# A graph layer's front on one core: the node table split into bf16 parts through TensorE, in spans of three nodes, under one written order

## The chip, the core and the metric

The kernel runs on one core of a Trainium2 chip. The core has TensorE (PE, matrix products, with its weight loads shown as PEld), VectorE (DVE), ScalarE (ACT), GpSimd (POOL) and SyncE (SP), which here only issues DMAs. The metric is the device time of one execution in microseconds (us); lower is better.

## The reference

One layer of a graph network over 12 500 nodes with 128 features and 200 000 edges of 4 types. The edges come sorted by destination, and low node numbers have far more of them (the destinations are drawn as the square of a uniform number).

```python
def reference(x, src, dst, edge_type_4, L0_gnn_W, L0_gnn_b):
    h = jnp.maximum(_layernorm(x, axis=-1), 0.0)      # per node, no learned scale
    xs = h[src]
    msgs = 0
    for i in range(4):
        mask = (edge_type_4 == i)[:, None]
        msgs = msgs + jnp.where(mask, xs @ W[i] + b[i], 0.0)
    return x + jax.ops.segment_sum(msgs, dst, num_segments=12500)
```

## The kernel before

**Data.** Edges are taken in chunks of 128, 1 563 in all. The normalised rows h are written once to a table in DRAM, `htab`. A row there is 768 bytes: the float32 value split into three bf16 parts, since TensorE's bf16 products of the three parts add up to nearly the float32 one. Node p·98 + j lies on partition p at place j (`NW` = 98 places; the last partition is short, so nodes from place `NL` = 54 on are loaded in three pieces, L186 to L188, and those before in one, L183).

**The dense part.** The first 512 chunks belong to the few nodes with many edges. For them the kernel counts, per destination, how often each source and type occurs (`count`: two one-hot tiles L924/L925 on VectorE, a product L936 on TensorE, the counts out through ScalarE L939), and multiplies the counts with the whole table (`multiply`, L976, with the table read back as `hs`). It needs *slots*: each destination's edges, one to a row. `prep_dense` prepares the edges' sources, types and destinations (L343 on), `make_slots` finds the slots: `first_chunk` (one-hots of L787, products of L796), then `pick_out` (L787, products L825 and L828, masks L837 to L842 on VectorE), then `unpack` (L851 on), then sums of the bias by L895 and L897.

**The other chunks.** The first 48 of them, three *raw groups* of `G` = 16 (`RAW` = 3), do not wait for the table: GpSimd gathers rows of x itself (`gather_raw`, L509, tile `hx`), VectorE takes their statistics (L431), ScalarE normalises them (L451), and TensorE sums them by destination and type in float32 (`add_up_raw`, L609 to L620). All later chunks take rows of the table by GpSimd gathers (`gather`, L525, tile `hm`, two chunks in each of 20 buffers), which need the whole table written. A group is summed by one-hots of its destinations (L542), products L559, a copy L562, the weights L586, and added into a ring (L637).

**Order.** In the loop (from L1182) the three engines PE, DVE and ACT run in the order in which the program writes their instructions (`tc.manual_schedule`), and the dense work is dealt out between the groups' parts by a pace. In front of the loop a scheduler orders the instructions; SP and POOL are always ordered by it. The first gathers of `hm` are spread by gates: the k-th buffer's first gather also waits for the k-th of a list of marked instructions (`marks`, in `make_slots` and `add_up_raw`).

**The table.** It is made in 13 blocks of up to `XG` = 8 nodes per partition. `look` loads a block (three ahead) and takes statistics: L431 for each node, then L434 to L439 on VectorE, a square root L440 on ScalarE, L441 and L442. `table` normalises each node with ScalarE (L451) and splits the block:

```python
nc.scalar.copy(h3[:r, :n, 0, :], h[:r, :n, :])                              # L471
nc.vector.tensor_sub(h[:r, :n, :], h[:r, :n, :], h3[:r, :n, 0, :])          # L473
nc.scalar.copy(h3[:r, :n, 1, :], h[:r, :n, :])                              # L474
nc.vector.tensor_sub(h3[:r, :n, 2, :], h[:r, :n, :], h3[:r, :n, 1, :])      # L476
nc.sync.dma_start(htab[...][:, j0:j1, :], h3[...])                          # L477
```

Beside it stand the loads and small preparations: `heads` and `brow` (where a chunk's sums go in the ring, L1105 and L1106), and the bias, split into bf16 parts and laid out row by row by twelve DMAs of 256 bytes (L1140).

Of the kernel before, what the change touches and what calls it, by code (L numbers as in the profile page):

```python
# [35 lines left out]
F32 = mybir.dt.float32  # L36
# [12 lines left out]
P = 128  # L49
EPS = 1e-5  # L50
XG = 8
# [21 lines left out]
def kernel(  # L73
# [269 lines left out]
    def prep_dense():  # L343
# [6 lines left out]
        n = slice(0, DENSE)  # L350
        nc.vector.tensor_single_scalar(first1, di[:, n, 0], 1.0, op=ALU.add)
# [5 lines left out]

        lo = prep.tile([P, QB, P], I32, name="sf")
        nc.vector.tensor_single_scalar(lo[:, n], si[:, n], float(-(-(1 << 16) // NW)), op=ALU.mult)
        nc.vector.tensor_single_scalar(lo[:, n], lo[:, n], 16, op=ALU.arith_shift_right)  # L360
        bk = prep.tile([P, QB, P], F32, name="rel")
        nc.vector.scalar_tensor_tensor(bk[:, n], lo[:, n], float(-NW), si[:, n], op0=ALU.mult, op1=ALU.add)
        over = prep.tile([P, QB, P], F32, name="key")
        nc.vector.tensor_single_scalar(over[:, n], bk[:, n], -0.5, op=ALU.is_lt)
        nc.vector.tensor_sub(what[:, 1], lo[:, n], over[:, n])
        nc.vector.scalar_tensor_tensor(bk[:, n], over[:, n], float(NW), bk[:, n], op0=ALU.mult, op1=ALU.add)
        nc.vector.tensor_scalar(over[:, n], ty[:, n], 1.0, float(P), ALU.add, ALU.mult)
# [20 lines left out]
    nc.vector.tensor_copy(iota_n, iota_d)  # L388
    ones_h = prep.tile([P, P], F16, name="ones_h")
# [30 lines left out]
    looked = []  # L420

    def stats(xt, n, r, what, tag, wide=XG):

        bufs = 4 if wide == XG else 2
        sums2 = what.tile([P, wide, 2], F32, name="mv" + tag, bufs=bufs)
        var = what.tile([P, wide], F32, name="var" + tag, bufs=bufs)
        rstd = what.tile([P, wide], F32, name="rstd" + tag, bufs=bufs)
        nmr = what.tile([P, wide], F32, name="nmr" + tag, bufs=bufs)
        st = what.tile([P, wide, 2, 3], F32, name="st" + tag, bufs=3 if wide == XG else 1)
        for k in range(n):  # L430
            last = nc.vector.bn_stats(st[:r, k].rearrange("p h s -> p (h s)"), xt(k))  # L431
        looked.append(last.ins)

        nc.vector.tensor_tensor(sums2[:r, :n], st[:r, :n, 0, 1:], st[:r, :n, 1, 1:], ALU.add)  # L434
        nc.vector.tensor_tensor(var[:r, :n], st[:r, :n, 0, 1], st[:r, :n, 1, 1], ALU.subtract)
        nc.vector.scalar_tensor_tensor(
            var[:r, :n], var[:r, :n], 0.25 * D, var[:r, :n], op0=ALU.mult, op1=ALU.mult
        )
        nc.vector.tensor_tensor(var[:r, :n], var[:r, :n], sums2[:r, :n, 1], ALU.add)  # L439
        nc.scalar.activation(rstd[:r, :n], var[:r, :n], AF.Sqrt, bias=eps[:r], scale=1.0 / D)  # L440
        nc.vector.reciprocal(rstd[:r, :n], rstd[:r, :n])  # L441
        nc.vector.scalar_tensor_tensor(  # L442
            nmr[:r, :n], sums2[:r, :n, 0], -0.5, rstd[:r, :n], op0=ALU.mult, op1=ALU.mult
        )
        return rstd, nmr

    def normalize(xt, h, n, r, of):

        rstd, nmr = of
        return [  # L450
            nc.scalar.activation(h(k), xt(k), AF.Relu, bias=nmr[:r, k : k + 1], scale=rstd[:r, k : k + 1]).ins  # L451
            for k in range(n)
        ]

    seen_x = {}

    def look(j0, j1, r):
        xt = npool.tile([P, XG, D], F32, name="xt", bufs=4)
        load_nodes(xt, j0, j1)
        seen_x[j0] = xt, stats(lambda k: xt[:r, k, :], j1 - j0, r, aheads, "t")  # L460


    tabling = []

    def table(j0, j1, r):
        n = j1 - j0
        xt, of = seen_x.pop(j0)
        h = npool.tile([P, XG, D], F32, name="h")
        h3 = npool.tile([P, XG, 3, D], BF16, name="h3")
        normalize(lambda k: xt[:r, k, :], lambda k: h[:r, k, :], n, r, of)  # L470
        nc.scalar.copy(h3[:r, :n, 0, :], h[:r, :n, :])  # L471
        yield True
        nc.vector.tensor_sub(h[:r, :n, :], h[:r, :n, :], h3[:r, :n, 0, :])  # L473
        nc.scalar.copy(h3[:r, :n, 1, :], h[:r, :n, :])  # L474
        yield True
        nc.vector.tensor_sub(h3[:r, :n, 2, :], h[:r, :n, :], h3[:r, :n, 1, :])  # L476
# [4 lines left out]
    def table_steps():  # L481
        for t in list(tabling):
            if next(t, None) is None:
                tabling.remove(t)

    tables = []
    for j0, j1 in ((0, NL), (NL, NW)):
        for j in range(j0, j1, XG):
            tables.append((j, min(j + XG, j1), P))
# [60 lines left out]
    def sum_up(t0, g, rows, oh, last):  # L550
# [3 lines left out]
        for i0 in range(0, g, SG):  # L554
            i1 = min(i0 + SG, g)
            ps = s_ps.tile([P, SG, P], F32, name="ps")[:, :, :K]
# [34 lines left out]
    def add_up_raw(t0, g, rows):  # L591
        win = window_of(C0 + t0)
        K = NT * win
        oh = npool.tile([P, G, KR], F32, name="ohf", bufs=2)[:, :, :K]
# [6 lines left out]
        row = lambda k: rows(k, 0)  # L601
        done = normalize(row, row, g, P, stats(row, g, P, aheads, "r", wide=G))
        if t0:
            marks.extend(done[g // 2 - 1 :: g // 2])
        sb = spool.tile([P, G * KM], F32, name="sb")[:, : G * K].rearrange("p (g t n) -> p g t n", g=G, t=NT)
        for i0 in range(0, g, SG):
            ps = s_ps.tile([P, SG, P], F32, name="ps")[:, :, :K]
            for i in range(i0, i0 + SG):
                nc.tensor.matmul(ps[:, i - i0, :], rows(i, 0), oh[:, i, :], start=True, stop=True)  # L609
# [784 lines left out]
```

## Time and profile before

| | |
|---|---|
| time, median of 3 runs | 1667.20 us (1661.71 to 1671.48) |
| the profiled execution's own time | 1657.39 us |
| its span in the profile | 1655.6 us, mean granted clock 0.959 |
| PE / DVE / ACT / POOL busy | 81% / 62% / 36% / 63% |
| last subtraction of the table (L476) ends | 100.8 us |
| first gather from the table (L525) | 104.25 us |
| first product of the dense work (L936) | 152.3 us |

Times in a profile count from the start of the span. Lines such as L976 are lines of the kernel; a group's row names the engine, the tiles (output <- inputs), the shapes, how often it occurs, its busy time, the mean of one instruction, and the idle time of its engine just before it with what ended that. The mean of one instruction includes its latency: many in a row follow each other faster than that.

### The profile page before, as it was taken

The numbers are of one execution on the slowest core, as the hardware profiler recorded it, in microseconds if no ns is written. First come the engines' busy times: TensorE is split into PE (matmuls) and PEld (weight loads), VectorE is DVE, ScalarE is ACT, GpSimd is POOL, SyncE is SP. The second block draws the span as 40 slices with busy tenths as digits, with TensorE's granted clock in tenths as the row PEclk, the third lists the DMA queues.
The fourth block names the chain that finished last, engine by engine and source line by source line (L and its number), as shares of the span: only waits on it lengthen the run. The fifth ranks groups of instructions, "written<-read, shape, count | busy, mean of one in ns | idle before, by whom it ended". The sixth has DMA issues, their size and how long they took to land.

```text
span 1655.6 us, 30447 instructions
## 1 busy us (share of the span) xinstructions
PE 1340.6 (81%) x9644; PEld 793.0 (48%) x9644; DVE 1032.7 (62%) x5197; ACT 600.4 (36%) x1993; POOL 1035.9 (63%) x1078
## 2 busy tenths in 40 slices
PE   0275788888878888888988889888888988897985
PEld 0152455545445555454545545554544554554554
DVE  9876889776766565555656555655556554773245
ACT  7861525233242433424233342332424324224111
POOL 7737666666666666666666666666666566666660
PEclk9996699999999999999999999999999899999998
DMA  7634356655555655555555555565555555555652
GB/s 234 190 104 122 90 175 177 174 165 149 166 158 167 183 166 170 175 177 165 176 171 171 171 171 152 172 183 162 170 161 165 155 162 161 173 164 159 183 167 72
DMA packets 137188, 270.25 MB, mean 163 GB/s; under 512 B 25818, under 2 KB 73868, under 8 KB 137021
## 3 DMA queue, kind: packets, MB, share of 16 engines
q1 hardware_dynamic: 87341, 166.44, 33.7%
q0 software_dynamic: 49680, 101.81, 21.8%
q8 instruction: 76, 1.25, 0.3%
q14 instruction: 91, 0.75, 0.2%
HBM read 252.12 MB, written 16.04 MB: 162 GB/s over the span
## 4 chain that ended last, share of the span: by engine, by line
PE 75%; issue 10%; DVE 7%; POOL 3%; ACT 2%; another core or an unknown queue 1%; DMA 0%; DVEq 0%; ACTq 0%; POOLq 0%
PE pa L976 43%; PE pt L936 12%; PE py L586 7%; PE ps L559 7%; POOL hx L509 2%; DVE o L925 2%; DVE o L924 1%; ACT counts L939 1%; PE py L577 1%; PE pt L992 1%; PE pt L662 1%; DVE ring L637 1%; PE pt L828 1%; ACT sb L562 1%
## 5 line engine op out<-in xcount | busy, mean ns | idle before, releaser
L525 POOL DMA_INDIRECT hm<-htab,srcT x1003 | 973.5, 971 | 560.7 <-issue 226.0
L976 PE MATMUL pa<-counts,hs 128*128 128x416 fp8e4 (+1 forms) x4116 | 920.5, 340 | 67.7 <-issue 57.7
L976 PEld LDWEIGHTS <-hs 128*128 128x128 bf16 x4116 | 391.1, 99 | 417.2 <-issue 181.9
L939 ACT ACTIVATE counts<-pt 128x392 uint16<-128x392 f32 x714 | 351.9, 503 | 397.6 <-PE pt L936 194.5
L936 PE MATMUL pt<-o,o 128*128 128x392 bf16 x1167 | 382.2, 341 | 95.2 <-issue 44.4
L925 DVE TENSOR_SCALAR o<-iota_n,hkT 128x392 bf16<-128x392 f16 x1167 | 383.7, 329 | 0.0
L542 DVE TENSOR_SCALAR oh<-iota_b,keyT 128x56 bf16<-128x56 bf16 (+8 forms) x1003 | 170.4, 261 | 258.9 <-PE pa L976 91.2
L562 ACT COPY sb<-ps 128x224 f32<-128x224 f32 (+8 forms) x251 | 99.5, 396 | 482.9 <-PE pt L936 178.0
L637 DVE TENSOR_TENSOR ring<-ring,py 128x14 f32 (+7 forms) x976 | 167.8, 172 | 106.8 <-issue 17.5
L559 PEld LDWEIGHTS <-hm 128*128 128x128 bf16 x3009 | 165.0, 99 | 107.2 <-issue 44.7
L559 PE MATMUL ps<-oh,hm 128*128 128x56 bf16 (+8 forms) x3009 | 189.7, 197 | 26.7 <-issue 25.6
L924 DVE TENSOR_SCALAR o<-iota_b,loT,byT 128x128 bf16<-128x128 bf16 x417 | 138.0, 331 | 84.8 <-PE pt L936 41.2
L936 PEld LDWEIGHTS <-o 128*128 128x128 bf16 x1167 | 113.7, 99 | 118.4 <-issue 37.8
L939 ACT ACTIVATION_READ_ACCUMULATOR counts<-pt 128x1 f32 x714 | 147.4, 206 | 0.0
L586 PE MATMUL py<-sb,wsb 128*128 128x224 f32 (+7 forms) x488 | 133.0, 414 | 3.8 <-issue 3.8
L920 DVE TENSOR_SCALAR o<-iota_b,loT 128x128 bf16<-128x128 bf16 x375 | 99.2, 265 | 48.6 <-PE pt L936 26.4
L924 DVE TENSOR_SCALAR o<-iota_b,loT 128x128 bf16<-128x128 bf16 x375 | 98.1, 261 | 46.7 <-PE pt L936 27.6
L586 PEld LDWEIGHTS py<-sb,wsb 128*128 128x128 f32 x488 | 90.1, 198 | 38.4 <-issue 17.0
L509 POOL DMA_INDIRECT hx<-in_x_dram,srcT x48 | 56.0, 1167 | 22.9 <-issue 13.4
L609 PE MATMUL ps<-ohf,hx 128*128 128x40 f32 x96 | 17.3, 338 | 50.3 <-ACT h L474 44.7
L581 ACT CAST cnt<-py 128x224 bf16<-128x224 f32 (+7 forms) x61 | 23.9, 392 | 76.2 <-PE pa L976 28.4
L451 ACT ACTIVATE h<-xt,nmrt,rstdt 128x128 f32<-128x128 f32 x98 | 40.7, 481 | 6.4 <-DVE h L476 5.4
(211 smaller groups left out, 542.7 us busy)
## 6 DMA issues: line engine op xcount, KB each, us to landing
hs<-htab SPq DMA_DIRECT2D x336, 384.0 KB
hm<-htab,srcT POOLq DMA_INDIRECT x1003
htab<-h SPq DMA_DIRECT2D x11, 768.0 KB
xo<-in_x_dram SPq DMA_DIRECT2D x23, 256.0 KB
out_dram<-xo SPq DMA_DIRECT2D x23, 256.0 KB
xt<-in_x_dram SPq DMA_DIRECT2D x6, 512.0 KB
hs<-htab SPq DMA_DIRECT2D x14, 192.0 KB
xt<-in_x_dram SPq DMA_DIRECT2D x5, 448.0 KB
```

The source lines that it names most:

```text
L525: one = nc.gpsimd.indirect_dma_start(out=hm[:, (i - h0) * D3 : (i - h0 + 1) * D3], out_offset=None, in_=htab, in_offset=bass.IndirectOffse ...
L542: nc.vector.tensor_scalar(oh[:, i, :], iota_b[:, :K], keyf[:, at : at + 1], None, ALU.is_equal)
L559: nc.tensor.matmul(ps[:, i - i0, :], rows(i, c), oh[:, i, :], start=(c == 0), stop=(c == 2))
L562: nc.scalar.copy(sb[:, i0:i1].rearrange("p g t n -> p g (t n)"), ps[:, : i1 - i0, :])
L586: nc.tensor.matmul(py[:, :g, :], wsb[:, t, :], sb[:, :g, t, :], start=False, stop=(t == NT - 1))
L637: nc.vector.tensor_tensor(to, to, of(i), ALU.add)
L920: nc.vector.tensor_scalar(o1, iota_b, loT[:, s : s + 1], None, ALU.is_equal)
L924: nc.vector.tensor_scalar(o1, iota_b, loT[:, s : s + 1], by, ALU.is_equal, ALU.mult)
L925: nc.vector.tensor_scalar(o2, iota_n, hkT[:, s : s + 1], None, ALU.is_equal)
L936: nc.tensor.matmul(pb, o1, o2, start=first, stop=last)
L939: nc.scalar.activation(counts[:, :, i * NT : (i + 1) * NT], pb.rearrange("p (b t) -> p b t", t=NT), AF.Copy, accum_out=both[:, i : i + 1],)
L976: nc.tensor.matmul(pa[:, : nv * NT], hs[:, j - j0, c * D : (c + 1) * D], counts[:, j, : nv * NT], start=(j == 0 and c == 0), stop=(j == NW ...
```

## The change

The table is made in 33 spans of `UN` = 3 nodes per partition (18 in one piece each, 15 in three pieces), loaded into the 20 buffers that later hold gathered rows, up to 14 spans ahead. Both subtractions go to TensorE: a bank of PSUM gets h (a float32 product with the identity), then minus part 0, then minus part 1 (bf16 products with the negated identity); ScalarE copies parts 0 and 1, and part 2 is copied by ScalarE for odd spans and by VectorE for even ones. The three parts of a span stand in three successive steps. Statistics are taken in groups of 2, 4, 5, 5, 5, 6 and 6 spans, one group ahead. From the table on, PE, DVE and ACT run in written order: one small step per span (of `prep_dense`, of `ring_rows` with the ring's rows and the bias), then slot steps at two spans in five. After the last span, the raw groups' steps and the other slot steps follow by a written list. Up to the loop's first gathers nothing else changes but the gates, which now name normalised raw rows first and then the last marks of the slots. In the loop only the shape in which a PSUM tile is asked for changes.

The diff, cut to what runs in the front:

```diff
@@ prep_dense: "yield True" between its steps (six parts)
@@ statistics, normalising and the table
-    def stats(xt, n, r, what, tag, wide=XG): ...
-    def normalize(xt, h, n, r, of): ...
-    def look(j0, j1, r): ...
-    def table(j0, j1, r): ...
+    def look(xt, n, tag, wide):
...
+        looks = [lambda k=k: nc.vector.bn_stats(st[:, k]..., xt(k)).ins for k in range(n)]
+        def spread(): ...   # the four small VectorE steps
+        def root():         # ScalarE's square root
+        def scales(): ...   # reciprocal and shift on VectorE
+        def normalize(k, h): ...
+        return looks, spread, root, scales, normalize
+    def load_span(u):
+        j0, j1 = spans[u]
+        xt = hpool.tile([P, HG * D3], BF16, name="hm").bitcast(F32).rearrange("p (j d) -> p j d", d=D)
+        load_nodes(xt, j0, j1)
+        return xt
+    banks = [(s_ps, "ps"), (s_ps, "ps"), (y_ps, "py"), (a_ps, "pa")]
+    def first_part(u, one):
+        n = spans[u][1] - spans[u][0]
+        h = npool.tile([P, UN, D], F32, name="h")
+        h3 = npool.tile([P, UN, 3, D], BF16, name="h3", bufs=5)
         for k in range(n):
+            one(k, h[:, k, :])
+        nc.scalar.copy(h3[:, :n, 0, :], h[:, :n, :])
+        pool, name = banks[u % 4]
+        ps = pool.tile([P, 512], F32, name=name)[:, : n * D]
+        nc.tensor.matmul(ps, ident, h[:, :n, :].rearrange("p j d -> p (j d)"), start=True, stop=False)
+        nc.tensor.matmul(ps, minus, h3[:, :n, 0, :], start=False, stop=True)
+        splits[u] = ps.rearrange("p (j d) -> p j d", d=D), h3, n
+    def second_part(u):
+        ps, h3, n = splits[u]
+        nc.scalar.copy(h3[:, :n, 1, :], ps)
+        nc.tensor.matmul(ps, minus, h3[:, :n, 1, :], start=False, stop=True, skip_group_check=True)
+    def third_part(u):
+        ps, h3, n = splits.pop(u)
+        if u % 2:
+            nc.scalar.copy(h3[:, :n, 2, :], ps)
+        else:
+            nc.vector.tensor_copy(h3[:, :n, 2, :], ps)
         nc.sync.dma_start(htab[...][:, j0:j1, :], h3[...])
@@ add_up_raw: the same instructions in steps, with "yield True" between them
@@ in front of the loop
+    ordered.enter_context(tc.manual_schedule(engines={PE, DVE, Activation}))
+    small = chain(dense_steps, ring_rows())
+    for gi, us in enumerate(group_of):          # groups of 2, 4, 5, 5, 5, 6, 6 spans
...
+        for i, u in enumerate(us):
+            while len(queue) < min(NU, u + 14):
+                queue.append(load_span(len(queue)))
+            first_part(u, lambda k, h: here[4](at_here[u, k], h))
+            if u:
+                second_part(u - 1)
+            if u > 1:
+                third_part(u - 2)
+            last = None
+            for l in more_looks[:each]:          # statistics of the next group
+                last = l()
+            del more_looks[:each]
+            while last is not None and len(raws) < min(NRAW, 3 + (u + 1) * NRAW // (NU - 4)):
+                raws.append(gather_raw(len(raws), last))
...                                              # next group's spread, root, scales
+            if u >= 3:
+                if next(small, None) is None and u * 2 // 5 > (u - 1) * 2 // 5:
+                    next(to_slots, None)
+    second_part(NU - 1)
+    third_part(NU - 2)
+    third_part(NU - 1)
...
+    for step in "0 s 0 1 s 1 0 0 s 2 0 0 s 2 0 s 1 1 s 1 1 0 s 1 2 2 s 2 2 1 s 2 s 2".split():
+        next(to_slots if step == "s" else groups[int(step)], None)
     for _ in to_slots:
         pass
...
-    gates.extend(marks[: 20 - 1])
+    gates.extend(ties + marks[len(marks) - (20 - 1 - len(ties)) :])
@@ the loop's manual_schedule starts before the table instead of here
```

More of the change, by code (lines that the diff above doesn't have):

```diff
@@ L50 @@
 EPS = 1e-5
-XG = 8
+UN = 3
 G = 16
@@ L1077 @@
     spent = 0.0
-    for a in tables[:3]:
-        look(*a)
+    queue = [load_span(u) for u in range(6)]
     NRAW = RAW * G // HG
     raws = [gather_raw(k, None) for k in range(3)]
+    dense_steps = prep_dense()
+    next(dense_steps)
     w3 = w.rearrange("t i o -> i t o")
@@ L1142 @@
+    second_part(NU - 1)
+    third_part(NU - 2)
+    third_part(NU - 1)
+    assert len(raws) == NRAW and next(small, None) is None
     win_raw = window_of(C0)
```

230 lines of the change are left out of this document (127 added, 103 removed).

## The prediction

> **What bounds the kernel now.** The page's first part comes first, and after it the busy time by stage.
>
> ```profile
> PE 1340.6 (81%) x9644; PEld 793.0 (48%) x9644; DVE 1032.7 (62%) x5197; ACT 600.4 (36%) x1993; POOL 1035.9 (63%) x1078
> ```
>
> Over the whole span TensorE is the fullest engine, but the change does not touch the loop that gives this row its figures: on every engine the loop's instructions follow in the same order before and after. Only the front differs. So I read the stages (columns: us, then busy us of PE, PEld, DVE, ACT, POOL, then granted clock, DMA share, GB/s).
>
> ```profile
> 10.60:100.80 90.20, 21.48 (x76) 14.91 (x77) 80.67 (x333) 77.15 (x171) 54.93 (x60) 1.00 0.62 197
> 100.80:152.30 51.50, 36.75 (x210) 20.30 (x209) 32.15 (x102) 15.69 (x47) 33.01 (x33) 0.86 0.29 80
> 152.30:195.00 42.70, 24.45 (x125) 10.35 (x125) 31.52 (x149) 21.94 (x87) 28.55 (x29) 0.54 0.37 109
> 195.00:1620.00 1425.00, 1235.08 (x9034) 730.65 (x9031) 859.84 (x4450) 477.33 (x1673) 911.79 (x941) 0.97 0.58 168
> ```
>
> The table is made from 10.6 to 100.8 us. There VectorE (80.7 of 90.2) and ScalarE (77.2) are both nearly full, TensorE is at 24%. From 100.8 to 152.3 come the rest of the raw groups and the slots, and no engine is full (TensorE 71%, VectorE 62%): that stage is a chain of steps. The whole front is 152 us, 9% of the span. What carries the table are these groups of 10 to 153 us (busy, mean ns of one, idle before):
>
> ```profile
> L451 ACT ACTIVATE h<-xt,nmrt,rstdt 128x128 f32<-128x128 f32 x98 | 40.7, 481 | 6.4 <-DVE h L476 5.4 <-issue 0.8 <-DMA xt<-in_x_dram 0.3
> L451 ACT ACTIVATE hx<-hx,nmrr,rstdr 128x128 f32<-128x128 f32 x48 | 19.5, 480 | 0.0
> L473 DVE TENSOR_TENSOR h<-h,h 128x1024 f32<-128x1024 f32 (+2 forms) x13 | 15.1, 1160 | 0.7 <-issue 0.7
> L476 DVE TENSOR_TENSOR h<-h,h 128x1024 bf16<-128x1024 f32 (+2 forms) x13 | 14.9, 1150 | 0.0
> L471 ACT CAST h<-h 128x1024 bf16<-128x1024 f32 (+2 forms) x13 | 12.8, 987 | 0.3 <-DMA htab<-h 0.2
> L474 ACT CAST h<-h 128x1024 bf16<-128x1024 f32 (+2 forms) x13 | 12.8, 986 | 3.8 <-DVE h L473 3.8
> ```
>
> The reader sees 30 us of subtractions on VectorE, 66 us of the table's own work on ScalarE, and 19.5 us of raw rows normalised, half of them (24 of 48) beside the table, the rest behind it. The timeline has the ends of the stages and three prices used below.
>
> ```profile
> 78.28 3.72 SPq L1140 DMA_DIRECT2D b<-b  x5
> ...
> 95.40 2.50 PE L620 MATMUL pa<-sb,wsb 128*128 128x160 f32 x8
> 99.63 3.95 ACT L451 ACTIVATE hx<-hx,nmrr,rstdr 128x128 f32<-128x128 f32 x10
> ...
> 123.87 1.35 PE L620 MATMUL pa<-sb,wsb 128*128 128x160 f32 x8
> 152.29 0.97 PE L936 MATMUL pt<-o,o 128*128 128x392 bf16 x2 [1.69 <-DVE o L924]
> ```
>
> The same eight float32 matmuls of L620 take 2.50 us at 95 and 1.35 us at 124: TensorE runs at half rate while the table is made, though the clock row says 1.00 there. The loop's first matmul of dense work starts at 152.29. That time is what the change can move; from there 1503 us follow that I leave as they are.
>
> **The change part by part.** The sum is for the profiled execution (1657.39 us, span 1655.6).
>
> ScalarE in the table. A normalise costs 0.386 us from start to start (ten in a row, 3.95 us with the last at its full 0.48). 98 of them stay: 37.8. The copy of 1024 columns takes 0.94 from start to start and that of 512 takes 0.51, which on a line puts 384 at 0.39: 33 first copies, 12.9. Copies from PSUM: 160 columns follow each other at 0.19, and one of 480 lasts 0.56 by itself (L1161, at 137 us), so 384 cost 0.38 to 0.50; I take 0.38, since nothing stands between them but their pitch: 33 second copies 12.5, 16 third ones (odd spans) 6.1; the upper end would add 5.9. Seven square roots of 0.2: 1.4. Sum 70.7, from the first normalise at about 10.5.
>
> VectorE loses 26 subtractions, 30 us, and gains 17 third copies, 17 x 0.45 (512 columns from PSUM take 0.60) = 7.7. With some 22 us net gone it no longer binds the table. Where the stall at L451 goes (5.4 us for the VectorE's late L476): to ScalarE itself, which is next late.
>
> TensorE gains 33 times one float32 product of 384 columns and two bf16 ones. By L620 (160 columns, two records each, 0.15 a record warm, 0.30 at 95 us) the float32 one is 0.7 us warm and 1.4 at half rate; bf16 by L825 (512 columns, 0.22 warm, 0.43 half) 0.16 or 0.33. So 1.0 to 2.1 us a span, beside ScalarE's 70.7 / 33 = 2.14: hidden warm, and just hidden at half rate.
>
> Waits of ScalarE that are new: the root of statistics group 1 stands ahead of span 1's normalises and comes when VectorE has done four spans of it, about 2.2 us; the like at span 4, 0.9.
>
> SP. Today the twelve small DMAs that lay out the bias (L1140) follow three different writes of the table, five, four and three of them, at 0.74 us each (the 78.28 row). Now all twelve stand in one row ahead of the write of span 10, and behind them an x load in three pieces (0.4 + 0.93 + 0.4 in the rows of L186 to L188). That is 12 x 0.74 + 1.7 = 10.6 us of SP. ScalarE's first copy of span 15 needs the buffer of span 10 back (five of h3), and so stops. SP has some 2 us of lead and the ring gives room for two spans more; the bounds are 3 and 9 us, I take 7, since the write itself needs another 2.6 us to land. After it SP passes a write and three pieces in about 2.1 us, ScalarE's own pace: 1 us more.
>
> The Trainium skill, "DMA: Bandwidth & Descriptors", section "Rules for kernel authors", says that many small transfers should be coalesced and that under 64 KB one pays mostly overhead. The bias pieces are 256 bytes and their rows show it; the spans' writes, at 295 KB, lie above that size, and by the rule only the burst counts, which is in the sum already.
>
> Slots beside the table. Steps of the slots now stand between spans on TensorE in written order. The first chunks at spans 16 to 21 cost up to 1 us each, mostly hidden; the twelve products of the first pick before span 31 cost 0.6 warm and 4.4 at half rate: 2. The last spans' tail of copies: 1.5. The end of the table: 10.5 + 70.7 + 2.2 + 0.9 + 7 + 1 + 2 + 1.5 = 95.8, against 100.8.
>
> Behind the table. All 48 statistics of the raw rows and 24 of their normalises lay beside the table; now all come after it, 18.5 us of normalises at 0.386. VectorE's list there is 3 raw groups of 4.6 (14), 4.8 of selections, 9.3 of masks, 10.5 of unpacking, 1.6, and one-hots 2.2: 42 us. That is the lower end. TensorE takes the steps in the order written: it waits at the first raw group, since ScalarE starts its rows only some 7 us behind the table and does the second group's before it copies the first one's sums (about 4 us lost), then at the end for the last slot counts (about 3). I take 49.5; before, this stage took 51.5 with that much of the raw work done ahead of it. All at half rate the 37 us of matmuls would be some 58.
>
> The loop starts at 95.8 + 49.5 = 145.3 instead of 152.3: 7.0 us less. Its first gathers wait for the table's last write (the stall of the gather at 104) and for marks in the slots; by the loop's start some 40 can be there either way, at 1.25 us each, so they move with it. 1657.4 - 7.0 = 1650.4; the profiled run lies 0.6% under the median of 1667.2, so the forecast is 1660 us. A measurement of this kernel can tell about 0.5%, or 8.3 us.
>
> **The rivals.** *ScalarE alone.* The bias burst is absorbed by the buffers (VectorE and SP having 2 us of lead and more), and TensorE warms up: 10.5 + 70.7 + 3.1 + 3 = 87, then 47: the loop starts at 134, 18 us earlier: 1649. For it: no row of before shows ScalarE waiting for a write for over 0.2 us. Against: before, a buffer holds eight nodes and the burst is split in three.
>
> *No change.* The table ends at 96 but the raw rows' statistics and normalises go back on the chain, TensorE idling through them: 96 + 55 = 151, within 3 us of before: 1666. For it: the stage 100.8 to 152.3 is a chain already.
>
> *Slower: TensorE at half rate through the whole front.* ScalarE's second copy of a span waits for that span's float32 product and subtraction, 1.4 + 0.33 = 1.7 us, while ScalarE has 3 x 0.386 + 0.39 = 1.55 us of other work in between: each span then waits 0.2 to 0.3, 33 times 8 us, with 4.4 instead of 2 for the pick: the table ends at 106, and 58 us behind it put the loop's start at 164, 12 us later: 1679. It decides from a float32 product of about 1.2 us on. For it: every row of TensorE from 71 to 103 us is at half rate, and the rate falls again at 132 after 3 us in which it was 45% busy. Against: before, TensorE is idle 76% of the table, after only about half.
>
> The Trainium skill, "TensorE: Matmul & The Clock Gate", Part 1, has a mechanism for this: half rate is the state at rest, about 3.4 us of sustained work lifts it, and an idle window brings it back. By that rule the near-gapless 2.1 us a span of half rate would lift the clock at once, and the gaps at full rate might drop it; the fall at 132 us without any window wholly idle speaks for a stricter gate than that.
>
> **How the numbers follow.** The forecast has 0.46, with its own range of 3 to 12 us less (PSUM copies, burst); about half of it lies beyond 8.3. ScalarE alone has 0.18, no change 0.12, half rate 0.24, whose price reaches from 5 to 14 us since it may hold for only part of the front. So faster 0.24 + 0.18 = 0.42, same 0.22 + 0.12 = 0.34, slower 0.24. The range runs from 18 us less to 10 more: 1648 to 1677, which leaves out the outer parts of the first and the last rival.
>
> **What would show it.** In the profile after: the last third copy at about 96 us (87, 106 for the rivals); a gap of 3 to 9 us on ScalarE near span 15, released by the table's write, with twelve small DMAs on SP just before; the float32 products at 0.7 or 1.4 us; ScalarE's raw rows behind the table; the first matmul of the dense work at 145. The loop from there 1503 us long: if it differs by more than 5 us, the prediction's frame is wrong.

## The result and the profile after

The changed kernel takes 1688.83 us (median of 4 runs, 1686.64 to 1692.96) against 1664.45 for the kernel before (4 runs): a ratio of 1.0144, 95% interval 1.0101 to 1.0186. It is 24 us slower; the forecast was 1660, with a range of 1648 to 1677. The profiled execution has a span of 1688.4 us, 33 us more than the profiled execution before (1655.6): that one was faster than each of its four timed runs (1657.39, lowest 1661.01), so differences read from the two profiles are some 8 us larger than the difference of the medians.

The busy time of the changed kernel by stage, from the profile (us, then PE, PEld, DVE, ACT, POOL, granted clock, DMA share, GB/s): the table, the stage behind it up to the first product of the dense work, the first batch up to the first product with the table's rows, and the loop.

```profile
10.60:102.00 91.40, 57.73 (x158) 23.58 (x159) 49.90 (x220) 74.53 (x185) 45.44 (x60) 0.83 0.60 193
102.00:188.00 86.00, 53.77 (x261) 36.32 (x258) 46.10 (x164) 27.14 (x79) 40.10 (x42) 0.67 0.21 59
188.00:218.50 30.50, 22.24 (x127) 9.39 (x127) 29.31 (x144) 21.65 (x87) 20.37 (x21) 0.64 0.43 130
218.50:1640.00 1421.50, 1239.65 (x8990) 729.27 (x8989) 862.82 (x4443) 475.39 (x1670) 906.49 (x935) 0.97 0.58 167
```

VectorE has indeed been relieved in the table (80.7 to 49.9 us), ScalarE is nearly as full as before (74.5 of 91.4 us, then 77.2 of 90.2) and the table ends no earlier. The loss stands in the second row: 86.0 us where the kernel before needs 51.5. From the first dense product on (188.0) 1500.4 us follow, where 1503.3 followed before; the 13 us that the first batch is shorter (30.5, before 43.5 from 152.3 to 195.8) more than cover the 10 us that the rest is longer.

What makes the second row long, from the timelines of ScalarE, TensorE and VectorE (start, us, engine, line, what, idle before with its releaser):

```profile
124.58 3.63 PE L629 MATMUL ps<-ohf,hx 128*128 128x40 f32 x16 [5.55 <-ACT hx L455]
...
132.46 1.26 PE L635 MATMUL ps<-ohf,pick_f 128*12 128x160 f32 x8
133.75 0.83 DVE L614 TENSOR_TENSOR ohf<-iota_f,keyT 128x640 f32<-128x640 f32 x1 [9.41 <-PE ps L635]
...
137.94 6.26 ACT L455 ACTIVATE hx<-hx,nmrr,rstdr 128x128 f32<-128x128 f32 x16 [8.08 <-DVE nmrr L450]
...
155.74 0.29 ACT L630 COPY sb<-ps 128x160 f32<-128x160 f32 x1 [9.06 <-remote]
165.61 0.29 ACT L630 COPY sb<-ps 128x160 f32<-128x160 f32 x1 [9.57 <-remote]
```

Two things are to be seen. First, a chain of waits: VectorE wants to write the third raw group's one-hots at 124.3 and needs the first group's buffer back, which TensorE reads last in L635, from 132.5 to 133.7; behind that one-hot write stands the third group's scale, so that ScalarE normalises it only from 137.9 on. Second, two gaps of 9 us on ScalarE that no engine in the profile ends ("remote"). ScalarE waits there for products of L629 that by their rows started at 146.7 and 148.4. TensorE's rows, whose ends are modelled, go on to 153.0 in the first gap and to 158.4 in the second; but no engine's row shows a wait that TensorE ended between 149.3 (VectorE's L865) and 155.7, nor between 155.7 and 165.6. I call such stretches pauses.

### The profile page after: what moved, and what is told of

It is laid out like the page before. It is cut to its first block, busy times and chain, and to the rows that moved or that the text cites. A ratio compares the mean times of both kernels' runs of the same rounds, so it can differ in the third digit from the quotient of the medians.

```text
span 1688.4 us, 30859 instructions
## 1 busy us (share of the span) xinstructions
PE 1404.8 (83%) x9776; PEld 822.6 (49%) x9776; DVE 1019.5 (60%) x5153; ACT 610.4 (36%) x2043; POOL 1027.0 (61%) x1078
## 4 chain that ended last, share of the span: by engine, by line
PE 73%; issue 9%; DVE 8%; ACT 5%; another core or an unknown queue 2%; DMA 1%; SPq 1%; POOL 0%; DVEq 0%; ACTq 0%; POOLq 0%
PE pa L999 41%; PE pt L959 12%; PE py L599 7%; PE ps L572 6%; DVE o L948 2%; ACT h L455 1%; DVE o L947 1%; ACT counts L962 1%; PE py L590 1%; DVE ring L660 1%; PE pt L685 1%; ACT sb L575 1%; DVE oh L555 1%; PE pt L1015 1%
## 5 line engine op out<-in xcount | busy, mean ns | idle before, releaser
L999 PEld LDWEIGHTS <-hs 128*128 128x128 bf16 x4116 | 393.0, 99 | 411.5 <-issue 179.4
L959 PE MATMUL pt<-o,o 128*128 128x392 bf16 x1167 | 382.7, 341 | 70.6 <-ACT counts L962 28.6
L660 DVE TENSOR_TENSOR ring<-ring,py 128x14 f32 (+7 forms) x976 | 167.7, 172 | 104.1 <-PE pt L959 24.2
L947 DVE TENSOR_SCALAR o<-iota_b,loT,byT 128x128 bf16<-128x128 bf16 x417 | 137.9, 331 | 79.5 <-PE pt L959 38.9
L522 POOL DMA_INDIRECT hx<-in_x_dram,srcT x48 | 46.9, 977 | 33.3 <-DVE stt L434 15.7
L455 ACT ACTIVATE h<-hm,nmrt,rstdt 128x128 f32<-128x128 f32 x98 | 41.2, 486 | 1.8 <-DVE nmrt L450 1.8
L629 PE MATMUL ps<-ohf,hx 128*128 128x40 f32 x96 | 19.5, 383 | 19.4 <-issue 7.6
```

The costliest lines, as they stand in the source:

```text
L660: nc.vector.tensor_tensor(to, to, of(i), ALU.add)
L947: nc.vector.tensor_scalar(o1, iota_b, loT[:, s : s + 1], by, ALU.is_equal, ALU.mult)
L959: nc.tensor.matmul(pb, o1, o2, start=first, stop=last)
L999: nc.tensor.matmul(pa[:, : nv * NT], hs[:, j - j0, c * D : (c + 1) * D], counts[:, j, : nv * NT], start=(j == 0 and c == 0), stop=(j == NW ...
```

## The experiments

Theory A: in the written order the engines wait for each other in turn behind the table. Theory B: TensorE itself (at half of its full rate, and in pauses) makes the stage long. Theory C: the split through TensorE is what costs. Later came G (the pauses come with runs of gathers) and M (the raw work should not have been moved behind the table). The runs were made on several chips and occasions, and the kernel before did not take the same time on all of them; so a kernel is compared by its ratio to the kernel before run beside it, and by the stages of its own profile. The ratio comes from all runs and can differ from the quotient of the two medians, by 0.23% in the worst row (e13). This table has the stages in us (behind: from the last part 2 to the first dense product; batch: from there to the first product with the table's rows).

| kernel | table ends | behind | batch | median / before | ratio (95%) |
|---|---|---|---|---|---|
| before | 100.9 | 51.4 | 43.5 | | |
| after | 102.5 | 85.5 | 30.5 | 1688.83 / 1664.45 | 1.0144 (1.0101 to 1.0186) |
| e1 scheduler behind the table | 116.1 | 63.6 | 32.5 | 1679.74 / 1664.71 | 1.0090 (1.0060 to 1.0121) |
| e2 three buffers of one-hots | 103.5 | 72.6 | 31.8 | 1670.67 / 1664.71 | 1.0037 (1.0015 to 1.0058) |
| e3 subtractions on VectorE | 108.5 | 85.1 | 32.6 | 1693.02 / 1664.71 | 1.0156 (1.0111 to 1.0200) |
| e4 gathers late | 101.4 | 70.6 | 81.7 | 1718.40 / 1664.71 | 1.0326 (1.0282 to 1.0370) |
| e5 scheduler in the whole front | 118.7 | 76.2 | 31.9 | 1692.22 / 1666.39 | 1.0171 (1.0142 to 1.0199) |
| e6 e2, bias late | 100.8 | 68.8 | 31.1 | 1668.27 / 1666.39 | 1.0021 (1.0000 to 1.0042) |
| e7 e2, no gates | 104.3 | 96.0 | 31.8 | 1696.59 / 1666.39 | 1.0204 (1.0173 to 1.0235) |
| e8 e2, idle products | 100.3 | 94.5 | 31.8 | 1693.79 / 1666.39 | 1.0180 (1.0148 to 1.0213) |
| b1 before, raw work behind | 95.5 | 82.6 | 31.9 | 1701.10 / 1692.51 | 1.0053 (1.0033 to 1.0073) |
| e9 e2 and e4 | 104.1 | 58.5 | 81.4 | 1732.41 / 1692.51 | 1.0252 (1.0215 to 1.0290) |
| e11 e6, raw work beside | 124.8 | 70.1 | 32.5 | 1716.50 / 1692.51 | 1.0149 (1.0118 to 1.0180) |
| e12 after, gathers paced | 102.2 | 74.1 | 43.1 | 1705.91 / 1688.78 | 1.0097 (1.0067 to 1.0128) |
| e13 e6, gathers paced | 104.7 | 62.8 | 42.5 | 1697.65 / 1688.78 | 1.0029 (1.0001 to 1.0057) |
| e14 e11, gathers paced | 125.7 | 55.9 | 43.7 | 1711.92 / 1688.78 | 1.0127 (1.0088 to 1.0166) |
| e15 e6, raw groups first | 91.7 | 55.5 | 29.5 | 1404.31 / 1406.23 | 0.9982 (0.9972 to 0.9992) |
| e16 e15, part 2 on VectorE | 91.2 | 56.8 | 30.2 | 1406.25 / 1406.23 | 1.0005 (0.9989 to 1.0021) |
| e17 after once more | 102.8 | 87.2 | 33.2 | 1709.27 / 1688.70 | 1.0120 (1.0079 to 1.0161) |
| e18 e6 once more | 102.1 | 70.2 | 31.9 | 1695.70 / 1688.70 | 1.0035 (1.0008 to 1.0061) |

**e1: the scheduler orders what lies behind the table.**

```diff
     third_part(NU - 2)
     third_part(NU - 1)
+    ordered.close()      # and opened again in front of the loop
```

> The changed kernel, with the written order ended after the table's last span: behind it the scheduler orders the same instructions up to the loop, as before the change. Theory A (in the written order the three engines wait for each other in turn behind the table: VectorE 9.4 us for the third group's one-hots, ScalarE's third group of normalises ahead of the first group's counts, TensorE behind both): the stage from the table's end at 102 to the first dense product shrinks from 84 us to about 55, the time by 20 to 30 us, to about 1662. Theory B (TensorE itself, at half rate and finishing nothing from 146 to 155 and from 156 to 165 us): the stage stays within 8 us of 84, the time within 8 us of 1688.

The stage shrank to 63.6 us, but the scheduler pulled work from behind the table in between its last spans, and the table ended 14 us later. Of the 22 us only 8 are left at the first dense product, and 0.5% of the time. A pause of 13.9 us (ScalarE's wait before L637, to 149.1) stands in these 63.6 us too. Half a hit for A: order matters, another order is not by itself the cure.

**e2: one buffer more for the one-hots.**

```diff
-        oh = rawp.tile([P, G, KR], F32, name="ohf", bufs=2)[:, :, :K]
+        oh = rawp.tile([P, G, KR], F32, name="ohf", bufs=3)[:, :, :K]
```

> The changed kernel with three buffers of the raw groups' one-hots (ohf) instead of two, and nothing else. Theory A: VectorE's wait of 9.4 us at 124 us goes, the third group is normalised 9 us earlier, and the time falls by 5 to 12 us. Theory B: the wait goes too, but TensorE still ends the stage: within 3 us of the changed kernel.

More than A asked for: the ratio falls from 1.0144 to 1.0037, some 18 us, from one number. VectorE writes the third one-hots at 125.6 instead of 133.8 and ScalarE's third group follows without a gap:

```profile
130.81 6.26 ACT L455 ACTIVATE hx<-hx,nmrr,rstdr 128x128 f32<-128x128 f32 x16
```

This row of ScalarE's timeline stands at 137.94 in the changed kernel. B is refuted as the main term; a pause of 7 us was still in this profile. The profiled execution was the slowest of the ten (1679.28, median 1670.67), so its stages may be on the long side.

**e3: the subtractions on VectorE again, all else as changed.**

```diff
-        nc.tensor.matmul(ps, ident, h[...], start=True, stop=False)
-        nc.tensor.matmul(ps, minus, h3[:, :n, 0, :], start=False, stop=True)
+        nc.vector.tensor_sub(h[:, :n, :], h[:, :n, :], h3[:, :n, 0, :])
...
-        (part 2 copied from PSUM)
+        nc.vector.tensor_sub(h3[:, :n, 2, :], h[:, :n, :], h3[:, :n, 1, :])
```

> The changed kernel with the two subtractions of a span on VectorE again (spans of three, the steps and their order as they are; no products in the table, no copies from PSUM; part 2 is written by the subtraction). Theory C (the split through TensorE is what costs): the table ends earlier than 102 and the time falls by 5 us or more. Theory A and B: VectorE gets 33 times two subtractions of 384 columns, about 30 us, ScalarE loses 16 copies, 6 us: the table ends within 4 us of 102, and the stage behind it stays at 84 (A) or shifts with TensorE's clock (B); the time stays within 6 us.

C is refuted. The table ends 6 us later (108.5) than with the split through TensorE, more than the 4 us that A and B allowed; the stage behind it is the same (85.1) and the time is not lower.

**e4: the first gathers held back.** The gates all name the last mark in the slots.

```diff
-    gates.extend(ties + marks[len(marks) - (20 - 1 - len(ties)) :])
+    gates.extend(marks[-1:] * (20 - 1))
```

> The changed kernel with every gated first gather of a buffer from the table held back to the last mark in the slots, so that almost no gathers run while the raw groups are summed. Rival to B (TensorE's two pauses of 9 us at 146 to 165 come from the gathers that run back to back from 140 to 165.6): the pauses go and the loop's first product comes 15 us or more earlier, though the loop then waits for its rows. Theory A or TensorE by itself: the first dense product stays within 5 us of 186, and the time rises by some 10 to 25 us for the late rows.

With the same order on the three engines, the first dense product comes at 172.0 instead of 188.0 and no gap is left at L630. GpSimd's timeline shows the edit:

```profile
107.21 0.95 POOL L538 DMA_INDIRECT hm<-htab,srcT  x1 [0.30 <-issue]
166.89 1.04 POOL L538 DMA_INDIRECT hm<-htab,srcT  x1 [58.73 <-DVE sel L890]
```

In the changed kernel the gathers run back to back from 140.2 to 165.6, and the second pause ends at 165.6. The rise in time is larger than expected (3.3% over before, against 1.4% for the changed kernel): the first batch lasts 81.7 us, and two pauses of ScalarE stand in it, 10 us to 189.6 and 18 us to 219.7, while the gathers run back to back.

**e5: the scheduler in the whole front.** The written order starts in front of the loop, as before.

> The changed kernel with the written order only from the loop on, as before the change: spans of three, the split through TensorE and all steps of the front are there, the scheduler orders them. Theory A (the written order is what costs): close to the kernel before, 1655 to 1672. If the loss lies in the spans and the split themselves, at 1680 or above, as the kernel whose order was free behind the table alone (1680).

At 1.0171 this is no better than the written order. Its ScalarE stands still three times, the longest here, while 40 gathers run from 121.6 to 171.4:

```profile
143.34 0.29 ACT L630 COPY sb<-ps 128x160 f32<-128x160 f32 x1 [8.24 <-remote]
162.92 0.29 ACT L630 COPY sb<-ps 128x160 f32<-128x160 f32 x1 [19.29 <-issue]
177.66 0.29 ACT L630 COPY sb<-ps 128x160 f32<-128x160 f32 x1 [14.26 <-remote]
```

So "the written order is what costs" fell as stated. What holds of A is the chain through the two buffers.

**e6: the bias's twelve DMAs behind the table's last write, with three buffers.**

> Three buffers of the raw groups' one-hots (the kernel at 1671), and the twelve small DMAs of the bias put behind the table's last write. The prediction's burst: ScalarE's wait of 4.5 us at 58 us, for the write that stood behind them, goes, the table ends 3 to 5 us earlier and the time falls by as much. If the wait was covered: within 2 us.

Ratio 1.0021 against 1.0037: the intervals overlap, so a gain of 0 to 5 us is all that can be said. ScalarE's wait for the write (4.5 us at 58) is gone from the profile, and a wait for TensorE of 4.2 us at 69 has come.

**e7: no gates, so that 40 gathers run back to back from 107 on, with three buffers.**

> Three buffers of one-hots, and no gates on the first gathers from the table, so that all 40 run back to back from the table's end at 103 to about 155. Theory G (a run of back-to-back gathers is what holds TensorE up for 9 us at a time, as the kernel with late gathers, which lost these pauses, suggests): the pauses now lie between 105 and 155, and none from 155 to the first dense product; the time goes up by 0 to 15 us. If the pauses belong to TensorE's own clock or to a place in its program: they stay at 146 to 166.

Half a hit for G. A pause of 15 us came earlier, where G put it, but the stretch behind it did not become free: from 146.0 to 162.8 the eight products of L851 start 1.4 to 3.5 us apart, and ScalarE waits 12.5 us for the last of them. With 2.0% over before, against 0.4% in e2, the time also rose by more than the 15 us that G allowed.

```profile
141.83 0.29 ACT L630 COPY sb<-ps 128x160 f32<-128x160 f32 x1 [15.28 <-issue]
...
163.68 0.49 ACT L630 COPY sb<-ps 128x160 f32<-128x160 f32 x2 [12.45 <-PE pt L851]
```

**e8: idle products to keep TensorE's clock up, with three buffers.** After each step, four products of 392 columns into a bank that nothing reads.

> Three buffers of one-hots, and four idle products of 392 columns on TensorE after each step behind the table (some 200 in all, 0.17 us each at full rate; nothing reads them). Theory B (half rate is what makes the stage long and comes with the pauses): the granted clock stays at 1.0 from 105 us on, no pause over 3 us, and the first dense product comes within 5 us of 176 in spite of 30 us more work. If the clock is not the cause: the pauses stay, and the time rises by 10 to 30 us.

A miss for B: the granted clock still fell to 0.5 from 119.6 to 136.7, pauses of 5.8 and 3.8 us stayed on ScalarE, and the stage took 94.5 us. TensorE's own timeline has one more, before one of the idle products:

```profile
116.72 0.83 PE L1228 MATMUL py<-iota_n,ones_h 128*128 128x392 f16 x4
127.22 1.47 PE L1228 MATMUL py<-iota_n,ones_h 128*128 128x392 f16 x4 [9.68 <-remote]
```

It begins at 117.5, with the granted clock still at 1.0, so this pause did not come from half rate; the clock fell 2 us after it had begun. And the semaphore that the product waits for is one that TensorE's own products count up.

**b1: the kernel before, all raw work behind its table.** Every raw statistic depends on the last L476.

```diff
             last = nc.vector.bn_stats(st[:r, k]..., xt(k))
+            if wide != XG:
+                held_by(last, ended[-1], "the raw groups wait for the table")
```

> The kernel before, with one change: every statistic of the raw groups waits for the last subtraction of the table, so that all raw work (14 us of VectorE, 18.5 us of normalises, 96 float32 products) lies behind the table, as in the changed kernel, in the scheduler's order. Theory M (moving the raw work behind the table is the loss, whatever the order and the split): the table ends 8 to 15 us earlier than 100.8, the first dense product comes at 165 to 190 instead of 152, and the time rises by 10 to 30 us. If the loss comes from the written order or the spans alone: the time stays within 5 us of before.

The table ends at 95.5 and the first dense product comes at 178.1, as M says. The whole loses 9 us (0.5%), just short of M's 10 to 30 and more than the 5 of its rival. But here too a pause of 17.4 us stands in the stage, and the first batch is short in return. The move alone costs something, less than half of the 24 us.

**e9: three buffers and late gathers together.**

> The changed kernel with both edits that moved the first dense product: three buffers of one-hots (176 instead of 188) and the first gathers held back to the last mark in the slots (172). If the ring's wait and the pauses under the gathers are two separate terms, they add: the first dense product at about 158 to 162, close to the prediction's stage of 49.5 us behind the table plus a few us. If they are the same stretch counted twice: at 170 or later. The whole time is worse than with the ring alone (about 1700), since the loop starts without rows.

58.5 us behind the table, first dense product at 162.6: together the two edits take off 27 us, and singly 13 (ring: 85.5 to 72.6) and 15 (pauses: 85.5 to 70.6), 28 in sum. They are two terms. Between e4 and e9, neither of which has a pause at L630, the third buffer alone is worth 12 us of the stage (70.6 to 58.5) and 0.7% of the time (1.0326 to 1.0252).

**e11: raw statistics, one-hots and normalises beside spans 14 to 31, with e6's edits.**

> Three buffers of one-hots, the bias's DMAs behind the table (the kernel at 1668), and the first two steps of each raw group (statistics, one-hots, normalises) put beside the table's spans 14 to 31 instead of behind it. Theory M: the table ends some 18 us later (119), for ScalarE's normalises, but the stage behind it shrinks by 25 us or more, so that the first dense product comes at 155 to 163 and the time is 1655 to 1663, below the kernel before. If raw work costs the same on either side: the first dense product stays at 168 to 175 and the time within 4 us of 1668.

ScalarE has no room there: the table ends at 124.8, the stage behind it still takes 70.1 (with pauses of 16.8, 7.2 and 4.7 us), and the ratio is 1.0149. M's cure fails in this table.

**e12, e13, e14: the first 31 gated gathers tied one by one to ScalarE's instructions**, in the changed kernel, in e6 and in e11.

```diff
-                if i == h0 and gates and t0 + i >= SOON:
+                if gates and t0 + i >= SOON:
...
-    gates.extend(ties + marks[...])
+    gates.extend(ties)      # normalises, copies of sums and counts, the slots' counts
```

> The changed kernel with one change: the first 31 gated gathers from the table are tied one by one to instructions of ScalarE behind the table (every fourth normalise of the raw groups, the copies of their sums and counts, the slots' counts), so that they cannot run back to back while TensorE is behind. Two buffers of one-hots as in the changed kernel. Theory G (a run of back-to-back gathers holds TensorE up): the pauses of 9 us go, the first dense product comes at 168 to 175 instead of 188, and since the rows are there by then the time falls by 8 to 18 us against the changed kernel, to a ratio to before of 1.004 to 1.010. If the pauses are TensorE's own: first product at 183 or later and the ratio stays at 1.014.

> The same tying of the gathers, with three buffers of one-hots and the bias's DMAs behind the table. Theory G and A together: first dense product at 152 to 162, the ratio to before 0.993 to 1.000 (the kernel without the tying: 1.002). If pauses remain: 165 to 172 and the ratio stays at 1.002.

> The last kernel with the raw groups' statistics, one-hots and normalises beside the table's spans 14 to 31. Theory M: the stage behind the table is shorter than the 62 us or so of the untied and unmoved order by 20 us or more, which pays for a table that ends at 120 to 125: first dense product at 155 to 162, within 4 us of the kernel it is made from. If the raw work is better beside the table: below 150. If it was the move that made that kernel slower (ratio 1.015) and not the pauses in it (17, 7 and 5 us): 170 or later.

e12 loses no time to pauses behind the table (first dense product at 176.3, just past the 168 to 175 of G) and its ratio is at the upper end of what G gave, 1.0097. e13 has none there either (167.5, some 5 us later than G and A asked for), yet its ratio is no better than that of the kernel without the tying, as the rival to G had it. From e12 to e13, run side by side, the third buffer and the late bias take 11 us off the stage and 8 us off the median. The table says why: the first batch takes 43.1, 42.5 and 43.7 us, like before's 43.5, where the untied kernels take about 32. The pauses are not gone, they have moved into the first batch: in e13 ScalarE waits there 4.5, 3.8 and 3.2 us with no releaser in the profile. e14, although paced, still shows pauses of 11 and 5 us behind the table and stays at 1.0127 with 181.6; the late table of e11 seems a loss of its own, as far as a stage with such pauses tells.

**e15, e16: the raw groups first in the written list; and part 2 always on VectorE.**

```diff
-    for step in "0 s 0 1 s 1 0 0 s 2 0 0 s 2 0 s 1 1 s 1 1 0 s 1 2 2 s 2 2 1 s 2 s 2".split():
+    for step in "0 0 1 s 1 2 s 2 s 0 0 s 0 0 s 0 1 s 1 1 s 1 0 s 1 2 s 2 2 s 2 1 s 2 s 2".split():
```

> Three buffers of one-hots, the bias's DMAs behind the table (ratio 1.002), and the written list behind the table changed so that the three raw groups' statistics and normalises come first and the slots' steps fill VectorE behind them. If what is left of theory A is ScalarE's late normalises (group 0 from 110, group 2 only to 136): all normalises are done by about 126, the first dense product comes at 152 to 160 instead of 170, and the ratio to before falls to 0.992 to 0.998. If the stage is bound by TensorE's own products at half rate and its pauses: first product at 165 or later, ratio 1.000 to 1.004.

> The same, with part 2 of every span copied by VectorE. ScalarE loses 16 copies of 0.38 us in the table, VectorE gains 17 us less what it has free (it is busy 49 of 89 us there). If ScalarE sets the table's pace: the table ends 4 to 6 us earlier (95 to 97) and the ratio falls by 0.002 to 0.004 against the kernel beside it. If the chain between the three engines sets it: within 0.001.

When these two ran, the kernel before took 1406 us (of this more in the last section), and ScalarE shows no pause in their fronts. e15 is 0.2% faster than before, at the edge of what was expected, with the first dense product at 147.2; e16 is the same as before. The table ended only 0.6 us earlier in e16, so ScalarE's 16 copies do not set its pace there. As neither the changed kernel nor e6 ran beside them, the gain of the order itself (e15 against e6) is not separated from its conditions.

**e17, e18: the changed kernel and e6 side by side once more.**

> The changed kernel once more, beside the kernel before and the next one on one chip, since the last chip showed no pauses of TensorE at all (its waits before the products of the dense part are 0.6 us in all instead of 67.7) and took 1406 us for the kernel before. If the loss belongs to the program (ring of one-hots, raw work behind the table): the same loss in us on any chip, 18 to 26 us over before. If the pauses made it: on a chip without pauses 0 to 10 us over before.

> Three buffers of one-hots and the bias's DMAs behind the table, beside the changed kernel on one chip. If the ring is the main term: 14 to 22 us below the changed kernel on any chip, within 5 us of before. If the ring only mattered together with the pauses: on a chip without them within 8 us of the changed kernel.

20.6 us over before, and 7.0 with the ring and the bias mended: the two edits are worth 14 us (1709.27 - 1695.70) here too, at the low end of the 14 to 22 expected; that leaves 7 us over before instead of the 5 allowed. The pauses were there again (13.5 and 8.2 us in the changed kernel), so that the changed kernel's loss without them stays untried.

## Why the prediction was wrong

**The frame held.** The loop's instructions are the same, and from the first dense product on 1500 us follow for the 1503 that were left as they are. (They hold a first batch shorter by 13 us and a rest longer by 10, so that the agreement to 3 us is partly luck.)

**The table: forecast 95.8, measured 102.0 to 102.5.** The prices of the copies and products came as worked out (the two records of a float32 product of 384 columns last 0.91 us together at full rate and 1.65 at half rate, the latency of the second included). The normalises were priced too low: the sum took 0.386 us for each, but part 0's copy reads what the last of a span writes, and starts 1.29 to 1.30 us after the first of three, not 1.16. In 33 spans that makes 4.3 us, where 6.7 were missing in all:

```profile
92.16 1.26 ACT L455 ACTIVATE h<-hm,nmrt,rstdt 128x128 f32<-128x128 f32 x3
93.46 0.51 ACT L481 CAST h<-h 128x384 bf16<-128x384 f32 x1
```

The bias burst was there, 7.57 us of SP and 4.5 us of ScalarE (taken: 7, bounds 3 and 9):

```profile
46.29 7.57 SPq L1155 DMA_DIRECT2D b<-b  x12
...
58.13 0.51 ACT L481 CAST h<-h 128x384 bf16<-128x384 f32 x1 [4.49 <-DMA htab<-h]
```

Not in the sum was a wait of ScalarE's root of 5.2 us, to 40.5, for VectorE's statistics, which had themselves stood still for 3.84 us before L438 (to 38.4, "remote"), and some smaller ones. The relief of VectorE brought nothing because ScalarE was the next to be full, as the prediction said.

**Behind the table: forecast 49.5, measured 85.5. This step failed.** It went through the waits of TensorE on ScalarE (seven us to the first normalises, then the order "second group's normalises before the first one's copies"), and both are in the trace (110.0; 124.25). It did not go through the buffers that VectorE writes. The ring of two one-hot tiles was already in the kernel before, where the scheduler spread the three groups over 65 us (L609 from 55 to 120) and it cost one wait of 1.4 us (VectorE's, for L614). With three groups in one stage it ties VectorE to TensorE's last use of the first group: 12 to 13 us of the stage (e4 to e9, e2) and 8 to 18 us of the time (8 in e12 to e13 and 14 in e17 to e18, both with the bias; 18 in e2, across occasions). In the kernel as changed that is the larger part of the loss. The remainder, 0.2 to 0.4%, is of the size that the raw work's move costs in the old kernel (b1, 0.5%); that it is the same thing was not shown. Even without the ring's wait and the pauses the stage takes 58.5 us (e9), 9 more than the forecast: TensorE waits 4.35 us for VectorE's mask at 110.6 and 5.55 for ScalarE at 126.2, where the sum took about 4 for the first raw group; the other 3 were not followed up.

**The pauses.** Another 14 to 15 us of the stage are the pauses (e4; e2 to e9). The trace of before shows them, too, in its first batch, where I had left that batch alone as common to both. Moving work under the gathers moved the pauses from the batch into the stage: +15 there, -13 in the batch. So far as the total shows (e12: 1.0097 against 1.0144, with overlapping intervals), they change the place of the loss more than its size.

**The rivals.** The slower one was priced by TensorE's half rate through the whole front: a table end of 106 and 58 us behind it, 1679. Half rate was there for parts of both stages (granted clock 0.83 and 0.67), the table ended at 102, and its place and its sign came nearest; its mechanism was at most a part of it. One reason given for it was misread: the products at 132.1 of before have 368 columns, not 512, and start 0.155 us apart, which is the full rate (0.217 for 512); the clock record falls at 137.7. By the Trainium skill, "TensorE: Matmul & The Clock Gate", Part 1, about 3.4 us of sustained work should lift the clock and an idle window drop it. The trace is in keeping with that in the table, where the clock records change every 3 to 14 us, but between 141.8 and 179.4 us it stayed at half although the rows have TensorE busy from 168.9 to 178.6 without a gap. The rule does not tell what the pauses are.

## What to carry to other kernels

When an edit draws work together that lay spread out, go through every buffer ring that this work uses, not only the engines' lists: a ring of two that hardly cost anything can make the writer wait for the last reader of the group before last. An order written out by hand pays for each such wait in full, since nothing is moved into the gap; one more buffer gave back most of what the whole change lost. And a stage that moves should be priced together with the one that follows it, since a cost under the gathers can simply change its place.

## What the runs showed of the hardware

While gathers run back to back, an engine can wait 5 to 19 us with nothing in the profile that explains it. Most of these pauses show as waits for TensorE, but VectorE has them too. Here is its timeline in e7:

```profile
133.40 0.29 DVE L434 BATCH_NORM_STATS2 str<-hx 128x6 f32<-128x128 f32 x1 [1.10 <-issue]
134.80 0.29 DVE L434 BATCH_NORM_STATS2 str<-hx 128x6 f32<-128x128 f32 x1 [1.11 <-issue]
136.20 0.29 DVE L434 BATCH_NORM_STATS2 str<-hx 128x6 f32<-128x128 f32 x1 [1.11 <-issue]
146.03 0.20 DVE L438 TENSOR_TENSOR mvr<-str 128x32 f32<-128x32 f32 x1 [9.53 <-remote]
```

The statistics, 0.2 us apart elsewhere, start 1.40 us apart, and L438, which reads nothing but them, starts 9.5 us after the last has ended. The semaphore that it waits for is counted up by VectorE itself, and the trace records steps of it at 141.81, 143.21, 144.61 and 146.00. So here the work was done, by its rows, and the word of it came late. That TensorE's pauses are of the same kind is suggested by e8 and not shown.

In the front the pauses follow the gathers: held back (e4, e9) the stage behind the table loses them and the first batch gets them, paced (e12, e13, though not e14) the stage loses them too, ungated (e7) they begin earlier and last longer. The granted clock reads 0.5 in those of the changed kernel, but one in e8 began at 1.0. The loading of program code does not explain the second pause of the changed kernel (to 165.6): from 149.3 to 169.9 us only the gathers moved data by DMA. What the gathers hold up is not settled.

The loop has such gaps as well, and whether they are there depends on where or when a kernel runs. Here are the rows of the product with the table's rows, in the kernel before and then in e15 (groups: busy, mean ns, idle before):

```profile
L976 PE MATMUL pa<-counts,hs 128*128 128x416 fp8e4 (+1 forms) x4116 | 920.5, 340 | 67.7 <-issue 57.7 <-ACT sb L562 4.4 <-ACT sd L986 4.0
```

```profile
L999 PE MATMUL pa<-counts,hs 128*128 128x416 fp8e4 (+1 forms) x4116 | 892.6, 337 | 0.6 <-ACT sd L1009 0.6
```

And e15's loop by stage, from its first product with the table's rows on (columns as above):

```profile
176.70:1343.30 1166.60, 1153.71 (x8991) 716.55 (x8990) 853.77 (x4444) 497.96 (x1669) 884.46 (x906) 1.00 0.66 201
```

TensorE is busy 99% of that loop (1153.7 of 1166.6 us) and 87% of before's (1229.0 of 1412.8), at the same 0.34 us a product. Beside e15 the kernel before took 1406 us, at all other times 1664 to 1693. Of the 246 us between the two loops 171 are idle time of TensorE (183.8 against 12.9) and 75 are busy time of the same number of products; the loop's program is the same, and what makes the difference was not found. The chip is not shown to be it: the runs list the same chip number for e15 (1406.23) and for b1 (1692.51). A change of 1% of this kernel can only be judged against the kernel before run beside it.
